# The first batch's q, k and v products of a diffusion-transformer block: from tile products to block products on pairs of tiles

## The chip, the cores and the metric

One core of a Trainium2 chip runs the whole program. The metric is the device time of one execution in microseconds (us). TensorE (PE in the profile) multiplies matrices, VectorE (DVE) and ScalarE (ACT) work element by element, GpSimd (POOL) does some of that too and issues transfers, and SyncE (SP) only issues transfers. PEld is TensorE's weight load. "Tile" below means 128 tokens.

## What is computed

Two batches of 2048 tokens with 576 features go through one transformer block whose norms are shifted and scaled by a condition vector. Cut to what matters here:

```python
mod = silu(c) @ w_ada + b_ada                      # six vectors of 576 for each batch
xn  = ln(x, 1e-6) * (1 + sc_msa) + sh_msa
qkv = (xn @ w_qkv + b_qkv).reshape(B, N, 3, 16, 36)
q, k, v = qkv[:, :, 0], qkv[:, :, 1], qkv[:, :, 2]
q, k = ln(q, 1e-5, qn_g, qn_b), ln(k, 1e-5, kn_g, kn_b)     # over each head's 36
o = softmax(q @ k.T * 36 ** -0.5) @ v
x = x + g_msa * (o @ w_proj + b_proj)
x = x + g_mlp * (gelu(ln2(x) @ w1 + b1) @ w2 + b2)
```

## The kernel before

The program goes through the batches in order: q, k and v of the first batch, its attention and projection, the same for the second batch, then the MLP. Sixteen tiles make one batch. This text is about the first stage, which ends where attention's first scores (L1536) begin.

A tile gets ready for its products in these steps. A load brings 128 rows of x into one of three buffers (L1026, issued by POOL). VectorE takes mean and variance (`rows_measured`, L277 and L279), ScalarE the root (L281), VectorE the reciprocal (L283), the normed rows (L288) and a transpose inside 32x32 squares (L1042, tile `squares`). Four transfers write the squares to a scratch tensor in DRAM (`turned`, L1047), and three read them back with features on the partitions (`xnt`, L1055 and L1057). ScalarE then scales and shifts (`input_modulated`, L1064, L393, L394), and POOL makes the remainder of the last 64 features (L395). This last chunk is multiplied in two rounded parts.

A product of one tile with the weights of q, k or v is `product(w, t)` (w is 0 for q, 1 for k, 2 for v): two halves of 288 output columns, each of four matmuls over 128 features (L1143) and two over the last 64 (L1145), into one of four PSUM buffers `s`. `biased` (L1158 for q and k, L1161 for v) adds the bias on VectorE and takes it out of PSUM. For q and k of a tile, side by side in `both`, `squared` (L1097, ACT), `head_scale` (L1102 sum per head on VectorE, L1105 root on ACT, L1107 reciprocal on VectorE, L1109 product on POOL) and `by_feature` (L1122 transpose on VectorE, four writes L1124 to the DRAM tensor `qk`) follow. Once four tiles of `qk` are written, twelve reads (L817, L819, on SP's queue) gather the first heads' queries and keys from it; VectorE brings them into the form that attention wants (L852 to L862).

The second batch's stage already works on pairs of tiles. `seven_products` takes a pair of tiles and one of q, k, v as a 2 by 2 block matrix product and needs seven block products in place of eight (L1229, the biases as matmuls L1231, the last chunk L1235). It needs sums of the tiles' blocks (`token_sums`, four POOL operations L1267 to L1270) and sums of blocks of the weights (`weight_sums`, `wq4_less`). `combined` adds the products up (one ScalarE copy, five VectorE operations L1253 to L1257). The products come in the order 1; 2 and 6; 5 and 7; 4 and 3, where 1 and 2 need only the first tile of the pair and 6 a token sum.

The weight sums (L966 for the full chunks, L970, L405 and L406 for the last) are made in the first batch's stage, one per tile from tile 6 on, and written to DRAM (L1000, L1003) for the second batch, after `kept` has written the weights (L993, L994) at tile 5.

The order of work on DVE, POOL and SP is the order in which the code is written; each engine and each queue goes through its rows strictly in that order, and a row that waits holds all that stand behind it. ACT's order in this stage is a scheduler's.

Of the kernel before, what the change touches and what calls it, by code (L numbers as in the profile page):

```python
# [8 lines left out]
F32 = mybir.dt.float32  # L9
# [22 lines left out]
def dit_block(  # L32
# [241 lines left out]
    def rows_measured(pool, xt):  # L274
        st = pool.tile([P, 2, 6], F32, name="st", bufs=2)
# [3 lines left out]
        nc.vector.bn_aggr(mv, st.rearrange("p a s -> p (a s)"))  # L279
        std = pool.tile([P, 1], F32, name="std", bufs=2)  # L280
# [5 lines left out]
    def rows_normed(pool, xt, repeated=True):  # L286
        mean, rstd = rows_measured(pool, xt)
# [469 lines left out]
    def block_of_small():  # L757
# [163 lines left out]
        def first_weights(then):  # L921
# [31 lines left out]
            raw_less = pool.tile([64, 3, HALF], F32, name="raw_less")  # L953
# [4 lines left out]
            def sum_made(i):  # L958
                for k in range(2):
                    one, other = (  # L960
                        (block(0, 1), block(0, 0)),
                        (block(1, 1), sums[:, 0]),
                        (block(1, 1), block(0, 1)),
                        (sums[:, 1], block(1, 0)),
                    )[i]
                    nc.vector.tensor_tensor(sums[:, i, k], one[:, k], other[:, k], ALU.subtract)  # L966

            def ends_less():
                rows = raw.rearrange("p (w a f) -> p w a f", w=3, a=2)
                nc.vector.tensor_tensor(raw_less, rows[:, :, 1, :], rows[:, :, 0, :], ALU.subtract)  # L970
                weight_parts(wq4_less, raw_less)
# [33 lines left out]
            summed = [  # L1005
                *(lambda i=i: (sum_made(i), i and sum_kept(i - 1)) for i in range(4)),
                lambda: (ends_less(), sum_kept(3)),
                less_kept,
            ]
# [24 lines left out]
        def tile_turned(xt, queue):  # L1034
            rows_normed(xs["pool"], xt, repeated=False)
# [51 lines left out]
        def inputs(b, weights, making, work, xnts, turned, loaded):  # L1087
# [3 lines left out]
            key_blocks = {3: (0, 4), 7: (4, 8), 11: (8, 12), NT - 2: (12, 14), NT - 1: (14, NT)}  # L1091
# [7 lines left out]
            def head_scale(t, w0=0, w1=2):  # L1099
# [5 lines left out]
                nc.scalar.activation(var, var, AF.Sqrt, bias=eps5, scale=1.0 / HD)  # L1105
                inv = work.tile([P, 2 * H], F32, name="inv", bufs=2)[:, :n]
# [1471 lines left out]
```

## Time and profile before

| | us |
|---|---|
| three runs | 3079.7, 3082.24, 3081.69 |
| median | 3081.69 |
| span of the profiled execution | 3078.1 |
| TensorE busy in it | 3046.4 (99%) |
| the first batch's tile products, the last 78 halves | 64.50 to 236.37 |
| the second batch's 21 pair products | 1111.35 to 1281.78 |

The span leaves out what lies around the program: the median of the runs is 3.6 us longer. TensorE's busy time is its share of the span. Each time in the views is counted from the start of the span. The granted clock of TensorE is a share of 2.4 GHz.

### The profile page before, as it was taken

What the parts mean: (1) busy time and instruction counts of PE and PEld (TensorE: products, weight loads), DVE (VectorE), ACT (ScalarE), POOL (GpSimd) and SP (SyncE); (2) the same over time, 40 slices, a digit from 0 to 9 for tenths busy, and PEclk for the clock granted to TensorE, in tenths of its full rate; (3) what the DMA queues carried; (4) which work ended last, traced back from release to release, by engine and by line L of the source; (5) the groups of instructions that cost most, each with busy time, mean ns of one, the idle gap of its engine ahead of it and who ended that gap; (6) DMA issues with size and microseconds to landing.
All of it is one profiled execution on the core that took longest, in us unless ns stands there. A gap on an engine that the chain in (4) does not pass through costs nothing.

```text
span 3078.1 us, 51241 instructions
## 1 busy us (share of the span) xinstructions
PE 3046.4 (99%) x19047; PEld 1899.8 (62%) x19047; DVE 1687.3 (55%) x2560; ACT 1494.8 (49%) x2913; POOL 975.3 (32%) x1231
## 2 busy tenths in 40 slices
PE   8999999999999999999999999999999999999998
PEld 6884333333333688633333333348888888999998
DVE  6773454444543566544444444436666664667766
ACT  2326666766666223466666666642655553000000
POOL 4650100132322445301101111103444454545544
PEclk9999999999999999999999999999999999999999
DMA  5773322333332454412222222245887887855554
GB/s 149 188 147 90 102 80 62 77 93 93 97 97 74 165 127 80 95 43 69 50 54 73 77 66 66 65 118 159 237 245 234 252 241 275 319 197 192 201 192 154
DMA packets 427466, 415.09 MB, mean 135 GB/s; under 512 B 231336, under 2 KB 355176, under 8 KB 419080
## 3 DMA queue, kind: packets, MB, share of 16 engines
q1 hardware_dynamic: 380928, 309.08, 34.0%
q0 software_dynamic: 36848, 97.33, 11.8%
q10 hardware_dynamic: 9432, 5.31, 0.7%
q8 instruction: 153, 2.51, 0.3%
q14 instruction: 105, 0.86, 0.1%
HBM read 246.36 MB, written 154.75 MB: 130 GB/s over the span
## 4 chain that ended last, share of the span: by engine, by line
PE 96%; DMA 2%; DVE 1%; ACT 1%; issue 0%; SPq 0%; POOL 0%; DVEq 0%; ACTq 0%
PE b L1549 30%; PE b L1536 20%; PE b L2408 12%; PE m L2152 11%; PE s L1143 7%; PE s L1229 5%; PE s L411 2%; PE m L2166 2%; PE b L2417 2%; PE one L2152 2%; PE s L1731 1%; PE s L1145 1%; PE s L1235 1%; DMA operands<-cs 1%; DMA xt<-in_x_dram 0%
## 5 line engine op out<-in xcount | busy, mean ns | idle before, releaser
L1540 ACT ACTIVATE pt<-b 128x512 f32<-128x512 f32 x2048 | 1057.2, 608 | 481.7 <-PE b L1549 266.3
L1549 PE MATMUL b<-pt,vt 128*64 128x512 f32 x4096 | 935.0, 598 | 1.8 <-ACT pt L1540 1.8
L1549 PEld LDWEIGHTS b<-pt,vt 128*64 128x64 f32 x4096 | 271.8, 136 | 583.9 <-issue 438.0
L1536 PE MATMUL b<-qm,km 32*128 32x512 f32 x4096 | 563.6, 613 | 0.0
L1604 DVE TENSOR_TENSOR ot<-b,ot 128x512 f32<-128x512 f32 x186 | 128.6, 692 | 554.3 <-PE b L1549 554.3
L1536 PE MATMUL b<-qe,ke 16*128 16x512 f32 x2048 | 420.0, 791 | 0.0
L1536 PEld LDWEIGHTS b<-qm,km 32*128 32x128 f32 x4096 | 190.4, 184 | 271.2 <-ACT pt L1540 209.1
L1143 PE MATMUL s<-wq,xnt 128*128 128x288 f32 x864 | 226.9, 406 | 2.1 <-ACT xnt L400 2.0
L2152 PE MATMUL m<-xnt,wb 128*128 128x256 f32 x864 | 210.6, 379 | 2.8 <-DVE cs L2186 1.8
L2425 ACT COPY one<-b 128x144 f32<-128x144 f32 x55 | 15.4, 279 | 405.9 <-PE b L2408 398.3
L2152 PE MATMUL m<-s,wb 128*128 128x256 f32 x864 | 210.0, 379 | 0.0
L1569 DVE RECIPROCAL den<-den 128x512 f32<-128x512 f32 x62 | 206.9, 3336 | 0.0
L1602 DVE COPY ot<-b 128x512 f32<-128x512 f32 x62 | 42.9, 692 | 262.7 <-PE b L1549 262.7
L1143 PEld LDWEIGHTS s<-wq,xnt 128*128 128x128 f32 x864 | 157.7, 190 | 37.9 <-ACT xnt L400 2.7
L2152 PEld LDWEIGHTS m<-s,wb 128*128 128x128 f32 x864 | 164.2, 190 | 22.3
L1536 PEld LDWEIGHTS b<-qe,ke 16*128 16x128 f32 x2048 | 106.6, 184 | 114.0 <-issue 113.3
L2152 PEld LDWEIGHTS m<-xnt,wb 128*128 128x128 f32 x864 | 158.8, 190 | 23.0 <-DVE cs L2186 2.8
L2190 ACT ACTIVATE cs<-cs,b_sb 128x512 f32<-128x512 f32 x144 | 100.5, 721 | 137.5 <-DVE cs L2185 137.3
L1806 POOL DMA_DIRECT2D spare<-in_x_dram x32 | 17.7, 554 | 445.9 <-DVE met L796 445.9
L2192 POOL TENSOR_TENSOR cs<-cs 128x256 f32<-128x256 f32 x72 | 59.3, 824 | 247.8 <-ACT cs L2190 247.8
L1064 ACT ACTIVATE xnt<-xnt,mod 128x128 f32<-128x128 f32 x244 | 100.0, 481 | 77.0 <-DMA xnt<-turned 52.0
L2179 DVE TENSOR_TENSOR cs<-m,cs 128x512 f32<-128x512 f32 x72 | 49.4, 687 | 147.0 <-PE m L2166 98.9
(359 smaller groups left out, 4540.5 us busy)
## 6 DMA issues: line engine op xcount, KB each, us to landing
operands<-cs SPq DMA_DIRECT2D x70, 896.0 KB
wb<-operands SPq DMA_DIRECT2D x37, 1152.0 KB
operand<-operands SPq DMA_DIRECT2D x19, 1152.0 KB
spare<-in_x_dram POOLq DMA_DIRECT2D x64, 288.0 KB, 3.2
x_dram<-spare POOLq DMA_DIRECT2D x64, 288.0 KB, 2.5
qm<-qk SPq DMA_DIRECT2D x256, 64.0 KB
den<-den_dram SPq DMA_DIRECT2D x124, 128.0 KB
spare<-x_dram POOLq DMA_DIRECT2D x37, 288.0 KB, 3.3
```

Source lines behind the costliest of these rows:

```text
L411: nc.tensor.matmul(outs[a], stationary(k, a), moving(k, a), start=(first and k == 0), stop=(not first and k == FULL - 1),)
L1064: nc.scalar.activation(part, part, AF.Identity, **affine(which, k, b))
L1143: nc.tensor.matmul(out_a, full[:, k, :], wq[:, k, f], start=k == 0, stop=False)
L1229: nc.tensor.matmul(out[m], x_[:, k, :], w_(k), start=k == 0, stop=k == 1 and m == 6)
L1536: nc.tensor.matmul(ps, k[r, keys], q[r, :], start=first, stop=not first)
L1540: nc.scalar.activation(pt[:, h, :], banks[2 * c + h], AF.Exp, scale=SCALE)
L1549: nc.tensor.matmul(acc[64 * h : 64 * h + 64, :], vt[:, v0 : v0 + 64], pt[:, h, :], start=pt is pts[0][0], stop=pt is pts[-1][0],)
L1569: nc.vector.reciprocal(den, den)
L1604: nc.vector.tensor_tensor(ot, acc, ot, ALU.add)
L2152: nc.tensor.matmul(out_m[m], wb[:, f, slot[m], k, :], moving[m](k), start=k == 0 and m in (1, 2, 5, 6), stop=k == 1 and m == 1,)
L2190: nc.scalar.activation(part, part, AF.Gelu, bias=b1_sb[:, g : g + 1])
L2408: nc.tensor.matmul(out_m[m], stationary[m][:, c, :], w[:, 7 * c + m - 1, :], start=a == 0 and c == 0, stop=ends and c == FULL - 1 and m no ...
```

## The change

In the first batch, q and k of tiles 4 to 15 and v of tiles 6 to 15 now go through `seven_products` on pairs: six pairs of k, six of q and five of v, 17 pair products in place of 34 tile products. Tiles 0 to 3, and v of 4 and 5, stay tile products. The body of the second batch's loop becomes `in_pairs`, which both batches call; `beside(t0, place)` puts the first batch's own work into the loop: the norms of the tiles to come (places 0 to 4 of a pair), the writes of the weights and of their sums, and the last weight sums (place 5 of pair 6).

Of the weight sums, those of k are made in the fill at tile 1 and 2, those of q at tiles 3 to 5, those of v in pair 6. One set is now four VectorE operations over 128x576 and three over 64x288. The biases come over five small transfers (`bias_asked`) and three VectorE operations (`bias_rows`) in place of fifteen, in both batches. `turned_qk` has two buffers in place of three. ACT's order is written by hand here too. The four writes of a tile's squares go through SP's queue from tile 7 on (`turned_now` and `tile_turned` with `nc.sync`), through POOL's up to tile 6.

```diff
+    def rows_taken_in(pool, xt):
...
+            def sums_made(w):
+                for i, (one, other) in enumerate((
+                    (block(0, 1), block(0, 0)),
+                    (block(1, 1), sums[:, 0]),
+                    (block(1, 1), block(0, 1)),
+                    (sums[:, 1], block(1, 0)),
+                )):
+                    nc.vector.tensor_tensor(sums[:, i, :, w], one[:, :, w], other[:, :, w], ALU.subtract)
+
+            def ends_less(w):
                 rows = raw.rearrange("p (w a f) -> p w a f", w=3, a=2)
+                nc.vector.tensor_tensor(raw_less, rows[:, w, 1, :], rows[:, w, 0, :], ALU.subtract)
+                weight_parts(wq4_less[:, w], raw_less)
...
-            key_blocks = {3: (0, 4), 7: (4, 8), 11: (8, 12), NT - 2: (12, 14), NT - 1: (14, NT)}
+            key_blocks = {3: (0, 4)}
...
-                turned_qk = work.tile([P, 2 * C], F32, name="turned_qk", bufs=3)
+                turned_qk = work.tile([P, 2 * C], F32, name="turned_qk", bufs=2)
...
-            for t in range(NT - 2):
-                modulated_ahead(t)
-                begun(t)
...
+            def keys_begun():
+                by_feature(3)
+                slots["due"] += [slots["now"] + 2 + i for i in range(len(taken))]
+
+            def beside(t0, place):
+                t = t0 + 3 + place // 3
+                if place == 0:
+                    if t0 == 8:
+                        kept()
+                    elif t0 > 8 and t0 < NT - 1:
+                        i = t0 - 10
+                        if i == 4:
+                            less_kept()
+                        else:
+                            sum_kept(i), sum_kept(i + 1)
+                elif place == 5:
+                    if t0 == 6:
+                        sums_made(2)
+                        ends_less(2)
+                elif t < NT and place in (1, 3):
+                    measured[t] = rows_taken_in(xs["pool"], loaded[t])
+                elif t < NT:
+                    turned[t] = tile_turned(loaded.pop(t), nc.sync, measured.pop(t))
+                    asked(t + 3)
+                if place == 2:
+                    features_begun(t)
+
+            with tc.manual_schedule(engines={mybir.EngineType.Activation}):
...
+                k = product(1, 1)
+                features_begun(4)
+                input_modulated(b, xnts[3])
+                turned_now(5)
+                asked(8)
+                biased(1, k, 1)
+                head_scale(0)
+                squared(1)
+                sums_made(1)
...
+                v = product(2, 3)
+                biased(2, v, 3)
+                head_scale(3, meanwhile=[lambda: sums_made(0)])
+                v = product(2, 4)
+                by_feature(2)
+                biased(2, v, 4)
+                ends_less(0)
+                v = product(2, 5)
+                more = token_sums(4)
+                keys_begun()
+                biased(2, v, 5)
+                return in_pairs(4, [], (sums, less, spread, ones), more, beside)
```

In SP's queue before, after the writes of the third tile's q and k (`qk<-turned_qk`, four to a tile), the weights are written, then the fourth tile's q and k, then the gathers of the first heads (L817, L819) begin:

```order
L1124 DMA qk_284<-turned_qk 32x36x32 x12
L993 DMA wq_kept<-wq 512x1x1152
L994 DMA wq_kept<-wq_258 128x1728
L1124 DMA qk_284<-turned_qk 32x36x32 x4
L817 DMA qm_218<-qk_284 32x512
L819 DMA qe_221<-qk_284 16x1x512
L817 DMA qm_218<-qk_284 32x512
L819 DMA qe_221<-qk_284 16x1x512
L817 DMA qm_218<-qk_284 32x512
```

In SP's queue after, the writes of all four tiles' q and k (sixteen) and the gathers (L823, L825, twelve) stand first; the first gather waits for the landing of the third and the fourth tile's writes. These are the last of the gathers and what stands behind them; `turned_857` is the squares of tile 7:

```order
L825 DMA qe_221<-qk_284 16x1x512
L823 DMA km_217<-qk_284 32x512
L825 DMA ke_219<-qk_284 16x1x512
L823 DMA km_217<-qk_284 32x512
L825 DMA ke_219<-qk_284 16x1x512
L1048 DMA turned_857<-squares 32x18x32 x4
L1327 DMA qk_284<-turned_qk 32x18x32 x7
L1048 DMA turned_962<-squares 32x18x32 x4
```

The writes of the squares of tile 7 and of the tiles behind it have moved into SP's queue, and those of tile 7 stand behind the twelve gathers.

In POOL's queue before, around the same writes (`turned_757` is tile 7 there, `xnt_712` tile 6's last features, L1109 a tile's product with the scales of its heads):

```order
L1047 DMA turned_757<-squares 32x18x32 x4
L1109 TENSOR_TENSOR both<-both,inv 128x1152
L395 TENSOR_TENSOR xnt_712<-tail,xnt_712 128x128
L1026 DMA x_first<-in_x_dram 128x576
L1055 DMA xnt<-turned_757 128x4x128
L1057 DMA xnt_800<-turned_757 64x128 x2
L1047 DMA turned_845<-squares 32x18x32 x4
```

In POOL's queue after, from the third tile's head product (L1112) to the read of tile 7's squares (`turned_857`); `more` are the token sums of tiles 4 and 5:

```order
L1112 TENSOR_TENSOR pair<-pair,inv 128x1152
L1048 DMA turned_716<-squares 32x18x32 x4
L1027 DMA x_first<-in_x_dram 128x576
L1112 TENSOR_TENSOR pair<-pair,inv 128x1152
L1282 TENSOR_TENSOR more<-xnt 128x256
L1283 TENSOR_TENSOR more<-more,xnt 128x256
L1284 TENSOR_TENSOR xnt<-xnt 128x256
L1285 TENSOR_TENSOR more<-xnt,more 128x256
L1056 DMA xnt<-turned_716 128x4x128
L1058 DMA xnt_807<-turned_716 64x128 x2
L1027 DMA xt_211<-in_x_dram 128x576
L1056 DMA xnt<-turned_857 128x4x128
```

POOL no longer writes tile 7's squares; it makes the token sums behind the fourth tile's head product and then issues the reads of tiles 6 and 7.

On VectorE before, at the fourth tile (index 3): sum per head, reciprocal, the bias of v, then the transpose of an earlier tile's q and k:

```order
L1102 TENSOR_REDUCE var<-sq 128x32
L1107 RECIPROCAL inv<-var 128x32
L1161 TENSOR_TENSOR vt<-s,bq 128x16x36
L1122 STREAM_TRANSPOSE turned_qk<-both 128x1152
L1158 TENSOR_TENSOR both<-s,bq 128x576
```

On VectorE after, at the same tile, up to the transpose of its q and k (the last row), which the last four of the sixteen writes send off:

```order
L1103 TENSOR_REDUCE var<-sq 128x32
L971 TENSOR_TENSOR weight_sums<-wq 128x2x288
L971 TENSOR_TENSOR weight_sums<-wq,weight_sums 128x2x288
L971 TENSOR_TENSOR weight_sums<-wq 128x2x288
L971 TENSOR_TENSOR weight_sums<-weight_sums,wq 128x2x288
L1110 RECIPROCAL inv<-var 128x32
L1125 STREAM_TRANSPOSE turned_qk<-pair 128x1152
L1164 TENSOR_TENSOR vt<-s,bq 128x16x36
L975 TENSOR_TENSOR raw_less<-raw_rows 64x288
L411 CAST wq_less<-raw_less 64x288
L412 TENSOR_TENSOR wq_less<-raw_less,wq_less 64x288
L1125 STREAM_TRANSPOSE turned_qk<-pair 128x1152
```

The four weight sums of q stand between the sum per head and the reciprocal that the fourth tile's head product on POOL waits for, and the rest of that set ahead of the transpose.

## Rows read from the trace of the kernel before

**Rows 1.** The page: the chain of work that ended last, shares of the span
```profile
PE 96%; DMA 2%; DVE 1%; ACT 1%; issue 0%; SPq 0%; POOL 0%; DVEq 0%; ACTq 0%
PE b L1549 30%; PE b L1536 20%; PE b L2408 12%; PE m L2152 11%; PE s L1143 7%; PE s L1229 5%; PE s L411 2%; PE m L2166 2%; PE b L2417 2%; PE one L2152 2%; PE s L1731 1%; PE s L1145 1%; PE s L1235 1%; DMA operands<-cs 1%; DMA xt<-in_x_dram 0
```

**Rows 2.** The chain of waits, 0 to 320 us: start us, us, what
```profile
64.50 1.94 PE s L1143 x8
...
234.16 1.94 PE s L1143 x8
```

**Rows 3.** The chain of waits, 1100 to 1290 us, the second batch's products
```profile
1111.35 0.97 PE s L1229 x4
...
1113.69 1.94 PE s L1229 x8
...
1281.78 1.06 PE b L1536 x6
```

**Rows 4.** VectorE's timeline, 45 to 95 us: start us, us, instruction, idle before and releaser
```profile
53.17 0.81 DVE L277 BATCH_NORM_STATS2 st<-xt 128x6 f32<-128x288 f32 x2
...
56.17 0.72 DVE L1158 TENSOR_TENSOR both<-s,bq 128x576 f32<-128x576 f32 x1
```

**Rows 5.** ScalarE's timeline, 48 to 115 us
```profile
56.92 1.16 ACT L1097 ACTIVATE sq<-both 128x1152 f32<-128x1152 f32 x1 [2.30 <-DVE both L1158]
...
69.83 1.65 ACT L1064 ACTIVATE xnt<-xnt,mod 128x128 f32<-128x128 f32 x4 [5.21 <-DMA xnt<-turned]
...
71.77 0.48 ACT L394 ACTIVATE tail<-xnt,mod 128x128 f32<-128x128 f32 x1
```

**Rows 6.** Groups by line, 17 to 250 us: mean ns behind the busy time
```profile
L1158 DVE TENSOR_TENSOR both<-s,bq 128x576 f32<-128x576 f32 x32 | 23.3, 733 | 15.4 <-PE s L1145 15.4
...
L1102 DVE TENSOR_REDUCE var<-sq 128x32 f32<-128x1152 f32 x14 | 18.7, 1335 | 0.0
L1122 DVE STREAM_TRANSPOSE turned_qk<-both 128x1152 f32<-128x1152 f32 x13 | 17.7, 1360 | 0.0
```

**Rows 7.** The weight sums' line: ns min/median/max, first and last start
```profile
L966 DVE TENSOR_TENSOR weight_sums<-wq,weight_sums x2: 1046/2178/3310, 137.5 to 140.7; 128x864 f32<-128x864 f32 x2
```

**Rows 8.** VectorE's timeline, 130 to 170 us
```profile
137.48 4.28 DVE L966 TENSOR_TENSOR weight_sums<-wq,weight_sums 128x864 f32<-128x864 f32 x2
```

**Rows 9.** GpSimd's timeline, 130 to 170 us
```profile
137.32 2.14 POOL L1109 TENSOR_TENSOR both<-both,inv 128x1152 f32<-128x1152 f32 x1
```

**Rows 10.** GpSimd's timeline, 1084 to 1135 us
```profile
1104.79 0.45 POOL L395 TENSOR_TENSOR xnt<-tail,xnt 128x128 fp32r<-128x128 f32 x1 [7.34 <-ACT tail L394]
1105.20 0.73 POOL L1267 TENSOR_TENSOR more<-xnt 128x256 f32<-128x256 f32 x1
```

**Rows 11.** SyncE's queue, its waits, 0 to 300 us: us, times, longest
```profile
SPq L817 <- DMA qk<-turned_qk: 8.3, 7, 3.7
```

**Rows 12.** SyncE's queue, timeline 90 to 130 us
```profile
118.08 0.32 SPq L817 DMA_DIRECT2D qm<-qk  x1
...
124.34 0.62 SPq L819 DMA_DIRECT2D ke<-qk  x1
125.61 4.14 SPq L1124 DMA_DIRECT2D qk<-turned_qk  x4
```

**Rows 13.** DMA issues, 60 to 130 us: KB each, median us to landing
```profile
xnt<-turned POOLq DMA_DIRECT2D x6, 256.0 KB, 4.6
turned<-squares POOLq DMA_DIRECT2D x20, 72.0 KB, 3.9
```

**Rows 14.** DMA issues, 98 to 104 us
```profile
turned<-squares POOLq DMA_DIRECT2D x4, 72.0 KB, 10.0
```

**Rows 15.** TensorE's waits, 1000 to 1060 us
```profile
PE s L1731 <- DVE vt L1762: 4.3, 1, 4.3
```

**Rows 16.** Windows: us, busy by engine, granted clock, DMA share, GB/s
```profile
1034.00:1039.00 5.00, 4.71 (x10) 3.42 (x11) 4.69 (x11) 0.00 (x0) 0.71 (x2) 0.50 0.55 174
1111.00:1282.00 171.00, 171.00 (x804) 139.86 (x805) 110.91 (x169) 56.93 (x123) 87.27 (x103) 1.00 0.46 83
```

More of the change, by code (lines that the diff above doesn't have):

```diff
@@ L1003, in less_kept @@
                 nc.sync.dma_start(out=saved["less"], in_=wq4_less.bitcast(F32))
[L1005 to L1009, printed above, removed]
+            summed = sums, wq4_less, sums_made, ends_less, sum_kept, less_kept
             return (wq, wq4, bq), close, (made, ends_made, bias_made, bias_spread, kept, summed)
@@ new lines, in turned_now, with bias_asked @@
+            def turned_now(t, queue=nc.gpsimd):
+                if t < NT:
+                    turned[t] = tile_turned(loaded.pop(t), queue)
+            def bias_asked():
+                rows, first = (work.tile([P, HALF], F32, name="one", bufs=2)[0:12, :] for _ in range(2))
+                nc.gpsimd.memset(first, 0.0)
+                for w0, src in ((0, saved["bq"]), (2, b_qkv[2 * C :])):
+                    n = src.shape[0] // C
+                    nc.gpsimd.dma_start(
+                        out=rows[4 * w0 : 4 * (w0 + n), :],
+                        in_=src.rearrange("(w f) -> w f", f=HALF).unsqueeze(1).to_broadcast([2 * n, 2, HALF]),
+                    )
+                    for w in range(n):
+                        at = 4 * (w0 + w) + 2
+                        nc.gpsimd.dma_start(
+                            out=first[at : at + 2, :], in_=src[w * C : w * C + HALF].partition_broadcast(2)
+                        )
+                spread = work.tile([P, HALF], F32R, name="bias_spread")
+                ones = work.tile([P, 6, P], F32R, name="ones")
+                nc.gpsimd.memset(spread.bitcast(F32), 0.0)
+                by_two = ident[:, 0:12].rearrange("p (j e) -> p j e", e=2)
+                nc.gpsimd.tensor_tensor(
+                    ones,
+                    *(by_two[:, :, e : e + 1].to_broadcast([P, 6, P]) for e in range(2)),
+                    ALU.add,
+                )
+                return rows, first, spread, ones
@@ L1198, in bias_rows @@
+            def bias_rows(rows, first, spread, ones):
+                up = high[0:12, :HALF]
+                nc.vector.tensor_tensor(rows, rows, first, ALU.subtract)
+                nc.vector.tensor_scalar(up, rows, sign_q[0:12, :], None, ALU.mult)
+                nc.vector.scalar_tensor_tensor(
+                    spread[0:12, :], rows, low_q[0:12, :], up.bitcast(F32), ALU.mult, ALU.add
+                )
                 return spread, ones
@@ L1277, in pair_opened @@
             def pair_opened(w, t0):
-                pairs[w] = work.tile([P, 2, C], F32, name="pair", bufs=4)
+                pairs[w] = work.tile([P, 2, C], F32, name="pair", bufs=4 if b else 3)
                 both.update({(w, t0 + t): pairs[w][:, t, :] for t in range(2)})
@@ L1367, in in_pairs @@
                 biased(2, v, 1)
-                rest = [qt]
-                for t0 in range(2, NT, 2):
+                return in_pairs(2, [qt], (sums, less, spread, ones), more)
+            def in_pairs(begin, rest, fixed, more, beside=lambda t0, place: None):
+                for t0 in range(begin, NT, 2):
                     last = t0 == NT - 2
-                    operands = sums, less, spread, ones, more
-                    for t in range(2):
+                    operands = *fixed, more
+                    beside(t0, 0)
+                    for t in range(2 if b else 1):
                         features_begun(t0 + 2 + t)
```

176 lines of the change are left out of this document (69 added, 107 removed).

## The prediction

> **What bounds the kernel now.** Start with the page's chain of work that ended last [rows 1]: 96% of the span is TensorE, with L1143, the first batch's tile products, at 7% and L1229, the second batch's pair products, at 5%. So a shorter product there shortens the span, as long as TensorE doesn't come to wait. Then the chain of waits by stage. In the first batch [rows 2] the pieces of eight L1143 matmuls follow each other from 64.50 to 234.16 us without another engine in between: 78 pieces, 77 steps, (234.16 - 64.50) / 77 = 2.203 us each. A product of one tile with one of q, k, v is two pieces, 4.406 us. In the second batch [rows 3] 21 pair products fill 1111.35 to 1281.78 us, 8.116 us each, again without a wait. Third, what feeds TensorE: the other engines' timelines and SyncE's queue, since in this stage they have slack now, and the change spends it.
>
> **The products themselves.** A pair product replaces two tile products: 8.812 - 8.116 = 0.696 us. Seventeen of them give 17 x 0.696 = 11.8 us. This price is firm: same shapes, same tiles, same PSUM buffers in both batches.
>
> **When TensorE wants what.** The three k products ahead of 64.50 stay where they are. Then come q, k, v of the fourth tile and v of the next two, 5 x 4.406 = 22.0 us, then k and q of pair 4, 16.2 us: pair 6 begins at 64.50 + 38.2 = 102.7. Its product 6 starts 1113.69 - 1111.35 = 2.34 us in [rows 3], so at 105.1. It needs a token sum, and this needs tile 7 scaled and shifted. Tile 7 is the first whose squares are written from SyncE's queue, and there they stand behind the last four writes of q and k, the landing of those, and twelve gathers. This is the chain that I price.
>
> **When VectorE lets SyncE go (T).** The writes of the fourth tile's q and k wait for its transpose. VectorE's rows up to it, with the shift and reciprocal of tile 5 as the start: on ScalarE the root of tile 5 now stands behind the squares of the first tile and the modulation of tile 3. The squares end at 56.92 + 1.16 = 58.08, a modulation takes 71.77 + 0.48 - 69.83 = 2.42 [rows 5], so 60.5, and the part of a norm chain behind the root is some 1.8 of its 56.17 - 53.17 = 3.0 us [rows 4], by estimate: 62.3. Behind that stand 4 biases of q or k and 2 of v at 0.73, 4 sums at 1.335, 4 transposes at 1.36 [rows 6], one norm chain at 3.0, 8 weight sums at two thirds of 1.046 [rows 7], and 13 small ones (288 columns or fewer) at 0.4, by estimate from the same row: 4.4 + 5.3 + 5.4 + 3.0 + 5.6 + 5.2, and 0.4 for a root waited for, 29.3 us. T = 91.6. That's the low end. The high end: a weight sum beside a head product of GpSimd took 3.31 us where the fastest took 1.046 [rows 7], and the pair of them stood 4.28 us from 137.48 while GpSimd's product ran from 137.32 for 2.14 [rows 8, 9]. Three places of the fill put such operations beside such products (weight sums of k, the bias rows, the last part of q's sums), at most 2.14 each: T = 98.0.
>
> **From T to the token sum (D).** Four writes 4.1 [rows 12]; their landing 3.7 at most, 1.2 as the mean (8.3 us in 7 waits) [rows 11]; twelve gathers, 118.08 to 124.96, 6.9 [rows 12]; four writes of half the size, 2.1 by estimate; their landing 3.9 as a median here [rows 13], 1.2 at best; the read back 4.6 [rows 13]; modulation 2.4 [rows 5]; the last features' remainder and two token sums 0.45 + 2 x 0.73 = 1.9 [rows 10]. Low 24.4, high 29.6.
>
> So product 6 of pair 6 can start between 116.0 and 127.6 where it is due at 105.1: **TensorE waits 10.9 to 22.5 us, and I take 17**, the middle. In it lies the shorter wait in pair 4: its token sums stand on GpSimd behind the fourth tile's head product, and that waits for a reciprocal behind the weight sums of q. Whatever TensorE loses there, it doesn't lose again in pair 6. Before the change the same writes stood in GpSimd's queue, and nothing of this lay on the path.
>
> Here the Trainium skill speaks the other way. "DMA: Bandwidth & Descriptors", section "Issuing engines are not separate DMA queues", says that transfers from SyncE, ScalarE or GpSimd all run on the same 16 engines, and that the choice of issuer saves only sequencer time. By that the move of the squares would cost about the issue of four writes, and the sum would be -11.8 plus some 2. The row on SyncE's gathers waiting for landed writes [rows 11] speaks against taking it so here: the issuer's queue holds what stands behind such a wait. I go by the row.
>
> **What follows the wait.** TensorE's clock: the one long wait near full load, 4.3 us [rows 15], was followed by 5 us at 0.50 of the full clock, 4.71 of them busy [rows 16], so half of that, 2.4 us, is lost once. The weight sums of v in pair 6 and the combining that has queued up by then can hold PSUM: 0 to 4 us (four sums at 0.7 and three small ones), I take 2. Pair 8 begins with the writing of the weights, ahead of q's writes and tile 11's squares in SyncE's queue. Before, squares caught in that burst landed in 10.0 us where 3.9 is usual [rows 13, 14], 6.1 more; with the weight sums' writes in pairs 10 and 12, up to 3 more: 0 to 9.1, I take 3.5, since the wait in pair 6 has let the norms run ahead.
>
> **Costed at nothing.** Adding up and norms on VectorE in steady pairs: in the second batch it is busy 110.9 of 171 us [rows 16] beside the same products, 15.8 of a pair's 24.4, and two norm chains add 6.0; if that cover fails, each pair costs what overflows. The second batch's bias operations, twelve fewer, lie beside tile products that don't wait: 0, with 2 us lost if the new small transfers come late. ScalarE's copies and GpSimd's token sums in steady pairs have the second batch's cover too.
>
> **Sum.** -11.8 + 17 + 2.4 + 2 + 3.5 = +13.1 us. Against the profiled execution's 3078.1 that is a span of 3091.2; the median lies 3.6 us over the span, so 3094.8, and I say 3095. Its own bounds: -11.8 + 10.9 + 2.4 = +1.5, and -11.8 + 22.5 + 2.4 + 4 + 9.1 = +26.2: 3083 to 3108.
>
> **Rivals.** Each is the same sum with other ends; 3081.7 is the median before. What a measurement of this kernel can tell from no change is 0.2%, 6.2 us, so "same" is 3075.5 to 3087.9.
>
> A, faster: SyncE passes tile 7's squares in time. It decides where T + D is at most 105.1 + 5.6 = 110.7, with D at its low end T at most 86.3, 5.3 us before my low end. It needs VectorE's rows to be shorter than their counts say, or the gathers to be let through earlier. For it speaks that TensorE has no wait in either stage now [rows 2, 3]; against it that each term of D is a queue's or a landing's own row. By this the time is 3081.7 - 11.8 to 3081.7 - 6.2, 3070 to 3075.5, about 3072. It is also what the skill's rule above would give.
>
> B, no change: VectorE goes by the low end (its two-operand operations miss GpSimd's products) and every landing is short, with nothing lost in later pairs: -11.8 + 10.9 + 2.4 = +1.5, 3083. For it speaks that the fastest of the same operation does take 1.046 [rows 7]; against it that three places have to miss.
>
> C, slower still: the burst of the weights' writing delays the squares of tiles 11, 13 and 15 by 6.1 each [rows 14] since they stand behind it in one queue, 18.3 in place of 3.5: 3095 + 14.8 = 3110. For it speaks that they now share the queue; against it that one burst passes in one pair and the later writes are smaller.
>
> **How the numbers follow.** Forecast 0.57, A 0.11, B 0.20, C 0.12. Faster 0.11, same 0.20, slower 0.57 + 0.12 = 0.69. The range leaves out A and the upper part of C: 3078 to 3108, which takes in B and the bounds of the forecast.
>
> **What would show it.** In the profile after: TensorE's waits list POOL's token sums at L1244 with one wait of 8 us or more near 105 us, and SyncE's queue shows the squares of tile 7 issued after 110 us; the granted clock falls to 0.50 behind it. Pair products at 8.1 us each where nothing waits show the gain. The fourth tile's transpose at 92 to 98 us shows T. If the squares are issued before 100 us and TensorE's waits in the stage add up to under 6 us, the chain is wrong and A holds; if attention, at 236 us before, begins later than 263 us, waits of later pairs were sized too small.

## The result, and the profile after

The changed kernel takes 3121.08 us, the median of four runs (3118.01 to 3124.11), the kernel before 3081.24 on the same chip: the ratio is 1.013, with an interval of 1.0116 to 1.0144. That is 39.8 us slower. Slower was forecast, at 3095 with a range up to 3108; the result lies 13 us beyond that range.

Below, "pair N" is the pair whose first tile is N: the pairs of the first batch are 4, 6, 8, 10, 12 and 14.

The page of the changed kernel answers to [rows 1]: the chain's shares, and the costliest group of L1244 (the pair products' matmuls), whose last column is the idle time of TensorE ahead of it and what ended it.

```profile
PE 90%; DVE 4%; DMA 2%; SPq 1%; issue 1%; ACT 1%; POOL 0%; DVEq 0%; ACTq 0%; POOLq 0%
...
L1244 PE MATMUL s<-wq,xnt 128*128 128x288 f32 x304 | 89.9, 423 | 19.0 <-ACT one L1273 17.8
```

TensorE has gone from 96% of the chain to 90%, and VectorE, ScalarE and queues have come in. The windows tell where (columns as in [rows 16]); the first is the pairs' stage, the second all that follows it.

```profile
89.00:281.00 192.00, 153.60 (x651) 121.07 (x649) 132.93 (x217) 50.41 (x112) 83.64 (x102) 0.89 0.60 130
281.00:3120.00 2839.00, 2823.66 (x18025) 1724.62 (x18025) 1497.00 (x2273) 1424.68 (x2756) 854.74 (x1063) 1.00 0.45 133
...
125.00:130.00 5.00, 3.37 (x7) 2.49 (x8) 3.55 (x7) 1.40 (x4) 4.10 (x7) 0.50 0.80 120
130.00:135.00 5.00, 5.00 (x21) 3.90 (x21) 2.75 (x5) 0.00 (x0) 2.17 (x2) 0.82 0.75 137
```

TensorE is idle 192.00 - 153.60 = 38.4 us in the pairs' stage, where before it wasn't at all [rows 2]. All behind it is unchanged: from attention's first scores to the end it is 3121.9 - 281.38 = 2840.5 us, before 3078.1 - 236.37 = 2841.7. So the loss lies ahead of attention, which begins 45.0 us later.

TensorE's waits from 0 to 300 us: us in total, times, longest.

```profile
PE s L1244 <- ACT one L1273: 17.8, 3, 10.4
...
PE s L1244 <- POOL more L1283: 9.6, 2, 6.8
PE s L1250 <- POOL xnt L401: 4.9, 1, 4.9
PE s L1244 <- DVE pair L1271: 3.8, 1, 3.8
```

The second and third row are the waits of pairs 4 and 6, which the prediction was about: 9.6 + 4.9. The first, in pairs 8, 10 and 12, it had not seen so.

The chain of waits, the end of the stage; it answers to [rows 2].

```profile
263.71 0.97 PE s L1244 x4
...
271.83 0.97 PE s L1244 x4
...
281.38 6.84 PE b L1595 x34
```

A pair product takes 271.83 - 263.71 = 8.12 us where nothing waits, as in the second batch [rows 3].

**The ledger.** Pair 4 begins at 89.69. Seventeen products of 8.116 us would end at 227.7; the last ends at 279.95, 52.3 us later. TensorE's waits are 37.3 of that (the 38.4 above hold also 1.1 of a gap of 1.4 ahead of attention). Half clock is another 12.1, by estimate: each window of 5 us from 85 to 285 us has (1 - granted clock) x busy time, and the sum is 12.1, in six places (90 to 105, 120 to 135, 150 to 160, 185 to 200, 220 to 230, 250 to 260 us). Some 3 us have no row. Against this stand the 11.8 us of shorter products. The profiled execution is also 2.7 us late from the start: its first load of x takes 15.17 us in the chain where it was 12.07 before. The matmul behind this load begins at 26.91 us, before the change at 24.19. In the profiles of the first eight kernels below, which have the changed kernel's code up to there, it begins between 24.09 and 26.62 us, so it scatters as much without any change.

### The profile page after: what moved, and what is told of

It reads as the page before. It is cut to its first block, busy times and chain, and to the rows that moved or that the text cites. A ratio compares the mean times of both kernels' runs of the same rounds, so it can differ in the third digit from the quotient of the medians.

```text
span 3121.9 us, 51392 instructions
## 1 busy us (share of the span) xinstructions
PE 3049.7 (98%) x19013; PEld 1899.3 (61%) x19013; DVE 1694.6 (54%) x2605; ACT 1500.2 (48%) x2926; POOL 981.4 (31%) x1238
## 4 chain that ended last, share of the span: by engine, by line
PE 90%; DVE 4%; DMA 2%; SPq 1%; issue 1%; ACT 1%; POOL 0%; DVEq 0%; ACTq 0%; POOLq 0%
PE b L1608 29%; PE b L1595 20%; PE b L2467 12%; PE m L2211 11%; PE s L1244 6%; PE m L2225 2%; PE s L417 2%; PE one L2211 2%; PE b L2476 2%; PE s L1790 1%; PE s L1250 1%; PE s L1146 1%; SPq L1327 1%; DMA xt<-in_x_dram 0%; DVE weight_sums L971 0%
## 5 line engine op out<-in xcount | busy, mean ns | idle before, releaser
L1865 POOL DMA_DIRECT2D spare<-in_x_dram x32 | 17.8, 557 | 448.1 <-DVE met L802 439.1
L1244 PE MATMUL s<-wq,xnt 128*128 128x288 f32 x304 | 89.9, 423 | 19.0 <-ACT one L1273 17.8
L1838 POOL DMA_DIRECT2D spare<-in_x_dram x32 | 17.4, 544 | 281.8 <-DVE met L802 273.9
```

The costliest lines, as they stand in the source:

```text
L1244: nc.tensor.matmul(out[m], x_[:, k, :], w_(k), start=k == 0, stop=k == 1 and m == 6)
```

## The experiments

All are the changed kernel with the edits shown; ratios are to the kernel before on the same chip.

**The late writes.** Pairs 8, 10 and 12 wait for a ScalarE copy (`one`, L1273, which takes the first product out of PSUM). What holds it in pair 8? SyncE's queue, ScalarE's and TensorE's timeline, and the windows (their last columns are the granted clock, the DMA engines' mean busy share and GB/s):

```profile
163.66 0.73 SPq L998 DMA_DIRECT2D wq_kept<-wq  x1
164.43 0.93 SPq L999 DMA_DIRECT2D wq_kept<-wq  x1
165.47 14.70 SPq L1327 DMA_DIRECT2D qk<-turned_qk  x7
180.27 2.13 SPq L1048 DMA_DIRECT2D turned<-squares  x4
```

```profile
188.55 1.65 ACT L1065 ACTIVATE xnt<-xnt,mod 128x128 f32<-128x128 f32 x4 [7.99 <-DMA xnt<-turned]
...
191.93 0.38 ACT L1273 COPY one<-s 128x288 f32<-128x288 f32 x1
```

```profile
192.36 2.29 PE L1244 MATMUL s<-wq,xnt 128*128 128x288 f32 x4 [10.39 <-ACT one L1273]
```

```profile
165.00:170.00 5.00, 5.00 (x25) 4.00 (x25) 3.86 (x10) 1.20 (x2) 2.79 (x5) 1.00 1.10 389
170.00:175.00 5.00, 5.00 (x26) 4.15 (x25) 4.64 (x8) 0.86 (x3) 0.30 (x1) 1.00 1.02 343
```

The weights' writes (L998, L999) go first. Seven writes of q and k behind them take 14.70 us, and tile 11's squares, which VectorE had made at 167.03, are issued at 180.27. ScalarE shifts and scales that tile at 188.55, and the copy for v, which stands behind this in ScalarE's hand-written order, comes at 191.93; TensorE has waited 10.39 us for it. In pairs 10 and 12, behind the writes of weight sums, the same writes of q and k take 9.24 and 8.77 us. While the weights are written the DMA engines are busy all the time, and transfers that GpSimd's queue issues then suffer too: from 163 to 175 us they land after 9.6 to 10.8 us, from 115 to 130 us after 2.6 to 3.5.

The first edit moves all these writes behind the last pair:

```diff
-                if place == 0:
-                    if t0 == 8:
-                        kept()
...
+                    beside(t0, 6)
...
+                if place == 6:
+                    kept()
+                    for i in range(4):
+                        sum_kept(i)
+                    less_kept()
```

> The changed kernel with one thing moved: the writing of the weights (at pair 8) and of their sums (at pairs 10, 12, 14) to DRAM comes after the stage's last pair. Theory W: those writes fill SyncE's queue and the DMA engines, so that the q and k writes behind them take 14.7, 9.2 and 8.8 us to issue in place of 3.7, and the next tile's squares behind those come late; TensorE's waits for ScalarE's copy (17.8 us in pairs 8, 10 and 12) go, and the clock drops behind them (some 2.4 us each): 3121 - 24 = about 3097, with up to 10 us back if the late writes collide with attention's first gathers. Theory S: the loop leaves the squares too little time in any pair, whatever stands ahead of them: under 6 us saved, 3115 or more.

Measured: 3120.11, ratio 1.013 (1.0113 to 1.0147). In the pairs it does what was expected: the seven writes take 4.07 us, and the waits for the copy fall from 17.8 to 1.3. But attention's first scores now wait, TensorE's and ScalarE's timelines:

```profile
275.88 2.68 PE L1594 MATMUL b<-qm,km 32*128 32x512 f32 x5 [12.11 <-ACT pt L1598]
```

```profile
273.94 1.28 ACT L1598 ACT_TABLE_LOAD   x1 [17.36 <-DMA wq_kept<-wq]
```

ScalarE stands 17.36 us until the weights are written, and TensorE 12.11, with windows at 0.50 behind it. The writes were the cause of the waits in the pairs, and at this new place they cost nearly as much (12.1 of waits and 2.6 of half clock): that the total can't be told from the changed kernel's says nothing against the cause. So the next edit puts them at other places, the weights into the fill behind the first tile's q and k, all sums into the last pair:

```diff
                 by_feature(0)
+                kept()
...
                 if place == 0:
-                    if t0 == 8:
-                        kept()
...
+                    if t0 == NT - 2:
+                        for i in range(4):
+                            sum_kept(i)
+                        less_kept()
```

> The changed kernel with the weights written in the fill, behind the first tile's q and k, and all weight sums in the last pair (none in pairs 8 to 12, none after the stage). In the run with all of them after the stage TensorE's waits for ScalarE's copy had fallen from 17.8 to 1.3 us, but attention's first scores then waited 12.1 us. If those writes are what holds the squares in pairs 8 to 12, both go: 3121 - 16 of waits - 3 x 2.4 of slow clock = about 3097. Rival: the burst collides in the fill just as well, with the squares of tiles 4 to 6, and the time stays above 3110.

Measured: 3106.0, ratio 1.0081 (1.0064 to 1.0098), 15 us less than the change, where 24 were expected. Attention begins at 263.03, 18.4 earlier. The seven writes of pair 8 take 4.10 us, the waits for the copy are 1.7, and half clock costs 5.1 in place of 12.1. What is short of the expected: small waits of up to 1.25 us in pairs 6 to 12, some 4 us more than in the changed kernel, and 3.7 us more from attention's start to the end, without a wait that the views show. Still, this is the largest single part of the miss.

**Pair 6's chain.** The twelve gathers, ahead of tile 7's squares in SyncE's queue, go behind them:

```diff
                 if place == 2:
                     features_begun(t)
+                    if t0 == 4:
+                        taken.extend([*take_q(0, 0), take_k_block(0, 4)])
...
-            key_blocks = {3: (0, 4)}
+            key_blocks = {}
```

> The changed kernel with the first twelve gathers put behind the writes of tile 7's squares in SyncE's queue. By the chain of the prediction a landing (some 2.4 us) and 6.9 us of gathers leave the path to pair 6's token sums: its waits of 4.9 and 2.8 us and the slow clock behind them go, 3121 - 10 = about 3111, and the later pairs' waits stay as they are. Rival: what is won in pair 6 is given back in pair 8, since tile 11's squares are late by a fixed time on SyncE: 3118 or more.

Measured: 3116.97, ratio 1.0121 (1.0104 to 1.0138). This interval overlaps the changed kernel's, so the total alone wouldn't show a gain; the stage's rows do. Pair 6's two waits, 4.87 and 2.84, become one of 3.36:

```profile
118.90 4.21 PE L1242 MATMUL s<-weight_sums,more 128*128 128x288 f32 x8 [3.36 <-POOL more L1281]
```

```profile
104.94 1.97 SPq L1048 DMA_DIRECT2D turned<-squares  x4
```

The gathers were a cause, but half as large as expected: attention begins 7.3 us earlier, 2.3 of them from an earlier start. TensorE's idle time from 85 to 285 us falls from 38.8 to 30.4, but what it loses to half clock rises from 12.1 to 16.2 by the same sum over windows. Free of the gathers, the squares stand on VectorE, which makes them at 104.14 behind pair 4's additions.

The first two token sums of pair 4 ahead of the fourth tile's head product on GpSimd:

```diff
                 biased(2, v, 3)
+                more = sums_begun(4)
                 head_scale(3, meanwhile=[lambda: sums_made(0)])
...
-                more = token_sums(4)
+                sums_ended(4, more)
```

> The changed kernel with the first two token sums of pair 4 put ahead of the fourth tile's head product on GpSimd. The wait of 6.8 us in pair 4 goes. By the prediction TensorE loses it in pair 6 instead, since that pair's token sums hang on SyncE's queue and not on TensorE: 3118 to 3121. Rival: the two waits add up, 6.8 us and the slow clock behind it saved: about 3112.

Measured: 3122.94, ratio 1.0137 (1.012 to 1.0154), close to the 3118 to 3121 expected.

```profile
121.64 0.61 PE L1250 MATMUL s<-wq,xnt 128*128 128x288 f32 x1 [9.02 <-POOL xnt L401]
```

Pair 4's wait falls from 6.77 to 3.40, and pair 6's grows from 4.87 to 9.02. TensorE loses this time once, in one pair or the other.

The squares through GpSimd's queue again:

```diff
-                    turned[t] = tile_turned(loaded.pop(t), nc.sync, measured.pop(t))
+                    turned[t] = tile_turned(loaded.pop(t), nc.gpsimd, measured.pop(t))
```

> The changed kernel with the squares of all tiles written from GpSimd's queue, as before the change. If SyncE's queue is what makes them late: tile 7's go out at about 108 us and not 114.5, tile 11's at 168 and not 180, the later ones 5 us earlier each: 3121 - 7 - 10 - 8 and some 7 of slow clock, about 3090. If the place in a queue costs only the issue of four writes: within 3 us of 3121. If GpSimd's own work holds them up as much: 3110 to 3121.

Measured: 3125.78, ratio 1.0148 (1.0131 to 1.0165), above all that was expected and nearest the third case. In pair 6 the long wait is gone (0.68 is left, 3.69 at the token sum). Pair 8 still waits 8.93 us for the copy, and pair 12 now 7.87. GpSimd's timeline:

```profile
173.53 0.75 POOL L1056 DMA_DIRECT2D xnt<-turned  x1 [11.69 <-PE s L1246]
...
176.21 2.65 POOL L1048 DMA_DIRECT2D turned<-squares  x4 [0.15 <-issue]
```

Tile 11's squares, made at 163.73, stand there behind the read of tile 10's, which had waited 11.69 us for TensorE to release a buffer. So either queue holds them, each for its own reason. What part in pair 8's burst is the queue's place and what part the bandwidth, this run doesn't separate.

**Put together.** The edits of the writes and of the gathers in one kernel:

> The same, and the first twelve gathers behind tile 7's squares. The gathers moved alone gave 4 to 5 us. If the two causes lie in different places of the chain they add up: 3097 - 5 = about 3092. Rival: what is won in pair 6 is lost in a later pair once the burst is away: 3097.

Measured: 3101.06, ratio 1.0063 (1.0047 to 1.008). The gathers are worth 5 us here, 4 when moved alone, so the two causes do add up; the level is 9 above what was expected, as it was without them. To these the token sums' edit, and ScalarE's copy ahead of the second tile's modulation:

```diff
-                        for t in range(2):
+                        for t in range(2 if b else 1):
                             input_modulated(b, xnts[t0 + 2 + t])
...
                     copied()
+                    if b == 0 and not last:
+                        input_modulated(b, xnts[t0 + 3])
+                        more = token_sums(t0 + 2)
```

> The same, with pair 4's first two token sums ahead of the fourth tile's head product, and ScalarE's copy for v ahead of the modulation of the next pair's second tile (token sums after it). The copy no longer waits for squares, the next pair's product 6 may: the small waits of pairs 8 to 14 go, some 2 us, and 3 to 7 in pairs 4 and 6: about 3086. Rival: token sums are then late for the next pair and each pair waits there: 3092 or more.

Measured: 3097.69, ratio 1.0056 (1.004 to 1.0073), the lowest of the pair versions, though by total it can't be told from the one before it and the one behind it. The time is the rival's, but not for the rival's reason: from pair 8 on no pair waits for token sums. TensorE's timeline, all waits of 0.9 us and over from pair 4 on:

```profile
95.95 4.21 PE L1242 MATMUL s<-weight_sums,more 128*128 128x288 f32 x8 [3.41 <-POOL more L1283]
...
116.88 0.40 PE L1248 MATMUL s<-wq,xnt 128*128 128x288 f32 x1 [1.69 <-POOL xnt L401]
120.88 4.21 PE L1242 MATMUL s<-weight_sums,more 128*128 128x288 f32 x8 [3.61 <-POOL more L1283]
...
144.48 2.26 PE L1242 MATMUL s<-weight_sums,more 128*128 128x288 f32 x4 [3.77 <-DVE pair L1269]
...
178.44 1.24 PE L1242 MATMUL s<-wq,xnt 128*128 128x288 f32 x4 [0.96 <-DVE vt L1266]
```

```profile
95.00:100.00 5.00, 4.05 (x9) 2.92 (x10) 4.97 (x7) 0.00 (x0) 4.04 (x4) 0.50 0.80 152
120.00:125.00 5.00, 4.12 (x9) 2.97 (x10) 2.61 (x5) 0.79 (x3) 4.38 (x6) 0.50 0.81 126
145.00:150.00 5.00, 5.00 (x14) 3.74 (x13) 4.97 (x9) 3.96 (x10) 2.02 (x4) 0.54 0.55 83
200.00:205.00 5.00, 5.00 (x25) 4.05 (x24) 4.89 (x10) 1.22 (x4) 4.66 (x7) 1.00 0.76 116
```

Behind 178.44, in the rest of pair 8 and in pairs 10 to 14, TensorE has one wait, of 0.83 us at 228.27, and the full clock: the steady state is nearly as fast as in the second batch. What is left lies in pairs 4 and 6: 3.41 + 1.69 + 3.61 + 3.77 = 12.5 us of waits, and 8.0 at half clock (the same sum over windows as above). This is more than the 11.8 us that the products save. Of the 18.2 us by which its profiled execution is longer than the one before the change, these are 20.5 - 11.8 = 8.7; 2.4 are a later start, 2.1 smaller waits, 1.4 the gap ahead of attention, 1.4 come behind attention's start, and some 2.2 have no row.

Tile 7's norm moved into the fill, its squares ahead of the last eight writes of q and k, with the writes, the gathers and the token sums as above and ScalarE's copy as in the changed kernel:

```diff
                 head_scale(3, meanwhile=[lambda: sums_made(0)])
+                turned_now(7, nc.sync)
+                asked(10)
```

> Writes apart, gathers late and the first two token sums early, and tile 7's norm in the fill, its squares ahead of the last eight writes of q and k on SyncE. By the prediction's chain the fourth tile's transpose, the last writes and their landing are then off the path to pair 6's token sums: its waits of 4.9 and 2.8 us go and the slow clock with them, 3121 - 24 - 11 = about 3085. Rival: VectorE's 3 us more in the fill come back as waits in pair 4: 3092.

Measured: 3100.26, ratio 1.0064 (1.0048 to 1.0081). Both figures missed. Of pair 6's waits one of 1.85 for its token sum is left, where the kernel above has 1.69 and 3.61, but others take their place: for VectorE (2.99 the longest) and once for GpSimd (1.65). That VectorE's part of tile 7's norm in the fill is the reason is argued from its order and not shown.

**A later start of the pairs.** The fill of the kernel before up to tile 9 or tile 7, and pair products from tile 10 (nine) or tile 8 (twelve):

```diff
+            BEG, done = 10, 3
+            for t in range(BEG):
...
+                if t >= done:
+                    q = product(0, t)
+                k = product(1, t) if t >= done else two_steps(1, t)
...
+            return in_pairs(BEG, [last_rows], (sums, less, spread, ones), more, beside)
```

> The kernel before with a part of the change: tile products and their order as before for tiles 0 to 9, pair products for q, k and v of tiles 10 to 15 (nine of them), the weight sums one set per tile at tiles 6 to 8 and their last rows at tile 9, the weights written at tile 5 as before, the weight sums in the last pair, squares of tiles 13 to 15 on SyncE's queue. The price of a pair product is 0.70 us under two tile products if nothing waits: 3080 - 9 x 0.70 = about 3074. If the pair loop in the first batch can't be fed at all, whatever stands in the fill, waits of pairs 10 to 14 as in the changed kernel (4 us each and slow clock) eat that: 3082 or more.

Measured: 3119.73, ratio 1.0128 (1.0111 to 1.0145). Both this kernel and the next scale and shift the features of the first pair's first tile twice. The fill has no wait, but from 161.78 on TensorE waits seven times for over 1 us, on VectorE and GpSimd. The longest, 10.43 us, is for an addition of VectorE (L1268). VectorE itself:

```profile
189.96 0.54 DVE L858 TENSOR_SCALAR km<-km,gb_at 64x512 f32<-64x512 f32 x1 [8.19 <-DMA km<-qk]
```

It stood 8.19 us for gathers of keys that this build puts directly behind the writes they read: a flaw of its own, so the run says little of the start's place.

> The same with pair products from tile 8 on (twelve), the weight sums at tiles 4 to 6, their last rows at tile 7, the weights still written at tile 5. If nothing waits: 3080 - 12 x 0.70 = about 3072. If the burst of the weights' writing now meets the squares of tiles 8 to 10, or the shorter fill leaves the norms too little time: a wait of some 4 us and 2 of slow clock, 3078.

Measured: 3118.52, ratio 1.0125 (1.0108 to 1.0142). Waits of 9.90 us for GpSimd's features and 7.83 for ScalarE's copy, of the same kinds as in the changed kernel, both in its first pair.

The same two starts with the norms one tile further ahead, the copy first and the gathers apart from their writes:

```diff
+                if BEG - 4 <= t < BEG - 1:
+                    turned_now(t + 4)
...
+            with tc.manual_schedule(engines={mybir.EngineType.Activation}):
+                head_scale(BEG - 1)
```

> Pair products from tile 10 on (nine) in the kernel before, with the norms one tile further ahead from tile 6 on, token sums of tiles 10 and 11 ahead of tile 9's products, weight sums at tiles 5 to 8, the first gathers of keys not waited for at once, ScalarE's order by hand in the pairs and its copy for v ahead of the next pair's second modulation. The losses of the changed kernel are put down to late norms, the writes in SyncE's queue and ScalarE's order; with these away nothing should wait over 1 us: 3080 - 9 x 0.70 + some 2 = about 3076. Rival: the pair loop loses more than 0.7 us per product in the first batch by itself, VectorE's norms beside it: 3080 or more.

Measured: 3105.13, ratio 1.0077 (1.0063 to 1.0091). This is the rival's side. TensorE's waits of 3 us and over, and VectorE's timeline:

```profile
165.12 0.61 PE L1246 MATMUL s<-bias_spread,ones 128*128 128x288 f32 x1 [3.29 <-DVE bias_spread L1210]
...
181.98 2.29 PE L1244 MATMUL s<-wq,xnt 128*128 128x288 f32 x4 [4.42 <-DVE pair L1268]
...
203.38 1.24 PE L1244 MATMUL s<-wq,xnt 128*128 128x288 f32 x4 [3.14 <-DVE vt L1268]
...
211.52 1.68 PE L1244 MATMUL s<-weight_sums,xnt 128*128 128x288 f32 x4 [3.33 <-DVE vt L1271]
```

```profile
157.99 3.61 DVE L975 TENSOR_TENSOR raw_less<-raw_rows 64x288 f32<-64x288 f32 x1
...
179.90 1.38 DVE L1125 STREAM_TRANSPOSE turned_qk<-pair 128x1152 f32<-128x1152 f32 x1 [4.00 <-DMA qk<-turned_qk]
...
199.12 1.38 DVE L1324 STREAM_TRANSPOSE turned_qk<-pair 128x1152 f32<-128x1152 f32 x1 [6.74 <-POOL pair L1320]
```

Now VectorE is late at each of them: a weight-sum operation at 3.61 us beside a head product of GpSimd, a transpose that waits 4.00 for one of the two `turned_qk` buffers, one that waits 6.74 for GpSimd.

> The same from tile 8 on (twelve pair products), norms one tile further ahead from tile 4 on, weight sums at tiles 3 to 6, the weights still written at tile 5. 3080 - 12 x 0.70 + 2 = about 3074. Rival: the burst of the weights at tile 5 meets the squares of tiles 8 to 10 and the shorter fill leaves a wait of 4 us or more with its slow clock: 3080.

Measured: 3107.3, ratio 1.0083 (1.0069 to 1.0096); TensorE's waits are 6.04, 4.84, 3.38, 2.73, 1.69 and 1.62 us, all of them for VectorE. No version came below the kernel before.

## Why the prediction was wrong, and where it was right

Slower came true, and the first long wait for the reason given. The size failed in one step, "What follows the wait": it put the slow clock and the writing of the weights at 2.4 + 3.5 = 5.9 us, and they took some 12.1 + 17.8 = 29.9.

**Right: what the change gives, and where it loses first.** The pair product is 8.12 us where 8.116 was taken. T, the fourth tile's transpose, starts at 99.81 and lets SyncE go at 101.2; less the 2.7 us of the late start that is 98.5, just past the high end of 91.6 to 98.0. It came out high for the reason that the high end gave, and at the three places it named: VectorE's operations were stretched beside GpSimd's work, as in [rows 7 to 9], by 3.6 us in the weight sums of k, 1.7 in the bias rows (L1209) and 1.2 in the last part of q's sums, there beside token sums. Here is the longest, and the same operation without GpSimd's work beside it:

```profile
69.56 4.36 DVE L971 TENSOR_TENSOR weight_sums<-wq,weight_sums 128x576 f32<-128x576 f32 x1
73.85 0.75 DVE L971 TENSOR_TENSOR weight_sums<-wq 128x576 f32<-128x576 f32 x1
...
99.81 1.38 DVE L1125 STREAM_TRANSPOSE turned_qk<-pair 128x1152 f32<-128x1152 f32 x1
```

GpSimd's product (L1112) ran from 71.17 us for 2.14, so the operation had begun 1.6 us ahead of it, while GpSimd was issuing transfers (67.87 to 71.15). The product alone doesn't account for 3.6 us, and no run shows what does; for this place the bound of 2.14 was too small.

D, from there to the second token sum, was put at 24.4 to 29.6. SyncE's and GpSimd's rows:

```profile
101.21 3.93 SPq L1127 DMA_DIRECT2D qk<-turned_qk  x4
107.53 0.32 SPq L823 DMA_DIRECT2D qm<-qk  x1
...
113.79 0.62 SPq L825 DMA_DIRECT2D ke<-qk  x1
114.52 2.05 SPq L1048 DMA_DIRECT2D turned<-squares  x4
```

```profile
118.77 0.76 POOL L1056 DMA_DIRECT2D xnt<-turned  x1 [10.08 <-DMA turned<-squares]
...
125.85 0.72 POOL L1283 TENSOR_TENSOR more<-more,xnt 128x256 f32<-128x256 f32 x1
```

The writes, their landing (2.4 us until 107.53), the gathers until 114.4, tile 7's squares, the read at 118.77, the sum's end at 126.57: D is 25.4. Pair 6's product 6 starts at 126.63 where it was due at 105.1, 107.8 with the late start: 18.8 us late, where 17 was taken; 14.5 of it are waits, the rest mostly half clock behind the first of them. As said, pair 4's 6.77 us are part of it. The sign of one wait of 8 us or more near 105 us did not come, since the lateness is split in three (6.77, 4.87, 2.84). The Trainium skill's rule, in "DMA: Bandwidth & Descriptors", section "Issuing engines are not separate DMA queues", that starting transfers on several engines at once saves only the time to issue them, would by the prediction's reading have made this 2 us; the rows don't agree with that reading: tile 7's squares were ready at 107.82 and issued at 114.52 behind the gathers, and where these were moved (3116.97) they were issued at 104.94.

**Wrong: the step "What follows the wait".** Its three terms were too small, two of them by far.

- The clock: 2.4 us, taken once, from one wait [rows 15, 16]. Measured some 12.1 in six places. The price of one fall was about right (12.1 / 6 = 2.0); the step counted one fall because it counted one wait.
- The writing of weights and sums: 3.5 within 0 to 9.1. Measured 17.8 of waits. With the writes elsewhere 1.7 were left, so some 16 belong to them. This was rival C's place, but that its 18.3 is near the measured 17.8 is luck: it took three delays of 6.1, and the waits were 10.39, 3.72 and 3.70. C had 0.12, on the ground that a burst passes in one pair and later writes are smaller. They were smaller, and so were their waits; but the burst of the weights alone cost more than the term's high end, and behind each of the two writes of sums the q and k writes took 9.24 and 8.77 us where 4.1 is usual, enough to make TensorE wait again. "The norms run ahead" was true and no help, since squares made at 167.03 stood in a queue until 180.27.
- The weight sums of v in pair 6: 2 within 0 to 4, measured 3.84. Besides the sums themselves (4.1 us of VectorE from 138.44), an operation of attention's setup took 3.20 us beside GpSimd's head product (L1320), 0.54 as the median:

```profile
145.34 3.20 DVE L858 TENSOR_SCALAR ended<-qe,gb_at 128x512 f32<-128x512 f32 x1
```

**Wrong: "Costed at nothing".** ScalarE's copies were given the second batch's cover. Its order here is written by hand, with the copy for v behind a modulation that waits for a transfer, so a late transfer reached TensorE through the copy. With the writes out of the way the cover nearly holds: with the changed writes and gathers no wait from 170 us on is over 0.82, and with the copy moved too 0.83 is the only one behind 178.44. No run moves the copy and leaves the writes in place. The bound for what would prove the prediction wrong was attention later than 263 us, waits of later pairs sized too small; it began at 281.38, and the runs show that reason. What was costed at nothing in the second batch did cost nothing: all behind the stage took 2840.5 us, before 2841.7. Rivals A and B are out: TensorE had to wait, and much longer than at B's low end.

By terms, against the sum of +13.1: waits of pairs 4 and 6 14.5 in place of 17, -2.5; clock +9.7; v's weight sums +1.8; later pairs +14.3; small waits 1.2; the gap ahead of attention's first score 1.4; pair 4 begins 0.5 later than its count; 2.9 without a row: 13.1 + 29.3 = 42.4, and attention does begin 45.0 - 2.7 = 42.3 later.

**What stays open.** Whether the pairs can be fed from the start: in the best version the first two still wait 12.5 us. How pair 8's burst divides between the queue's order and the transfers' bandwidth: the fully busy DMA engines and the late landings of GpSimd's own transfers speak for the second having a part. And whether the buffers matter that the change took away or left out (two of `turned_qk` for three, three of `pair` where the second batch has four): in the changed kernel's views VectorE waits for neither, and no run gives them back.

## What to carry to other kernels

A steady state that is faster says little of a stage that is short: price the first pairs, where the feeding engines have the fill's work left over, and count the half clock for each wait of some microseconds (2 us on the mean here), not once for a stage. When a queue takes over transfers, list all that stands ahead of each of them in every later round too, large background writes above all, and follow a late transfer through the engine whose hand-written order stands behind it. A write moved out of one stage's way has to be looked for at the next stage's start.

## What the runs showed of the hardware

- The clock fell behind waits shorter than the 4.3 us of the one known before [rows 15, 16], and length alone did not decide. In the version with pairs from tile 10 and norms ahead, waits of 3.29, 4.42 and 3.33 us have windows of 5 us at 0.50, 0.66 and 0.71 at their end or behind them, while one of 3.14 and two of 1.3 have 1.00. With tile 7's norm in the fill one of 1.85 has 0.84 and 0.82 (the first row below, windows 115 to 125); with the writes behind the last pair one of 3.72 has 1.00 (the other two rows):

```profile
117.09 2.94 PE L1242 MATMUL s<-weight_sums,more 128*128 128x288 f32 x8 [1.85 <-POOL more L1283]
...
149.72 1.21 PE L1244 MATMUL s<-weight_sums,more 128*128 128x288 f32 x4 [3.72 <-DVE pair L1271]
...
150.00:155.00 5.00, 5.00 (x25) 4.11 (x24) 4.97 (x9) 1.96 (x4) 3.90 (x6) 1.00 0.54 72
```

- In the changed kernel the slow clock added some 12.1 us to 37.3 of waits, 2.0 for each of the six falls.
- The same VectorE operation over 128x576 took 4.36 us beside GpSimd's work, 2.14 of it a product, and 0.75 alone. "SBUF — State Buffer" of the Trainium skill, section "Who interferes with whom", says that a VectorE instruction with two inputs in SBUF contends with a GpSimd instruction that reads SBUF; the trace agrees that the two slow down together, though here the operation had begun ahead of the product. An operation with one tile as its input also took 3.20 us beside such a product (L858, above), and another 2.11 where it takes 0.36 in the second batch (L1209, 12x288).
- Seven writes of q and k took 14.70 us of SyncE's queue behind the weights' writes, and 4.07 where these had been moved away. During the weights' writes the DMA engines' busy share was 1.10 and 1.02, and transfers from GpSimd's queue landed after 9.6 to 10.8 us.
